# The output bias of an attention layer: from a product of ones to an add of a spread-out row

## Chip, cores and metric

The kernel runs on one core of one Trainium2 chip. The metric is the device time of one execution in microseconds (us); below, the time of a kernel is the median of several executions.

## What is computed

The reference is a small network on x of shape (8, 512, 512) with a context of shape (8, 512, 384), all in float32. It has four blocks, each added to its own input:

```
x = x + xattn0(layernorm(x), ctx)     # cosine similarities of two projections
x = x + ffn0(layernorm(x))            # quantised linear, depthwise conv, silu, linear
x = x + xattn1(layernorm(x), ctx)     # 16-head attention
x = x + ffn1(layernorm(x))            # gated feed-forward with squared relu
```

The change is in the third block, the 16-head attention (head size 32):

```
q = x @ w_q + b_q;  k = context @ w_k + b_k;  v = context @ w_v + b_v
weights = softmax(q k^T / sqrt(32))           # per head
out = weights @ v                              # 512 x 512 per batch
return out @ w_o + b_o
```

What is added to the residual stream is out @ w_o + b_o. The bias b_v passes through the softmax unchanged (the weights of a row add up to 1), so the kernel folds it in: it uses the row b_v @ w_o + b_o, 512 numbers, as the bias of the output projection, the same row for each of the 8 x 512 tokens.

## The kernel before

The program is one static instruction list for each engine. It is written out at build time by a planner, the class `Agenda`. Every piece of work is a Python generator, a task. A task yields what it wants next: an engine with a cost in us (`"P"` TensorE, `"V"` VectorE, `"W"` VectorE for operations that share a port with Pool, `"A"` ScalarE, `"G"` Pool, `"S"` SyncE, which issues all DMAs), a buffer of a `Kind`, an `Event`, or a plain waiting time. The planner keeps a clock of its own, hands each engine to the wanting task with the lowest rank (`ag.me.rank`, a due time in us), and so fixes the order of instructions on each engine. On the chip that order is never changed; an instruction whose data isn't there holds up all those behind it on its engine. If a cost changes or a step is added, the planner deals out the order of everything that follows anew.

Where a step could run on two engines, the task yields a list and the planner takes the one with the smaller burden: the work queued before it and its own cost, weighed by `LOAD`. For ranks over 600 the weights are 2.5 for VectorE and 0.7 for Pool. The helper `tensor` is the one that matters here; most of VectorE's and Pool's instructions carry line L363, that of the wrapper `Ported`:

```python
def tensor(out, a, b, op):
    n = a.free_size() / 512
    way = yield [("W", 0.07 + 0.53 * n), ("G", 0.16 + 1.07 * n)]
    (V, G)[way].tensor_tensor(out, a, b, op)
```

The planner treats `"W"` and `"G"` work as taking turns at one port (`Agenda.port`). `Ported` adds to a Pool operation a wait for VectorE's last `"W"` operation planned before it.

Buffers in the on-chip memory come from 25 pages of 8 KB per partition (`main`); in the traces they are all called "main". Product results lie in 8 banks of 128x512 floats ("bank").

The work runs in four phases, one for each block, which overlap by rank: the third is due from 620 us (`R3`), the fourth from 1260 us (`R4`). In the third phase:

- Queries, keys and values go through DRAM (qd, kd, vd) and come back as stacks per group of 4 heads. There are 32 such head groups (8 batches of 4), each due 19 us after the one before (`T3`).
- For each head group, `maxima` makes 16 products (L1424) whose row maxima VectorE takes (`maximum3`, a TENSOR_REDUCE from a bank); `attention` makes 16 products of scores (L1488); ScalarE takes their exponentials (L1496) into pairs of tiles of 128x1024.
- `summed` adds these pairs over the keys, with `tensor`: operations of 128x1024 on Pool or VectorE.
- `weigh` makes the products with the values (L1536) and `sums` those that add the sums over partitions (L1554). `finish3` divides (the sums pass through DRAM, sd) and splits the result into two parts for the projection, `split_sb`, again with `tensor` at 128x512.
- `projections3` makes the output projection: for each batch, and each of its 4 tiles of 128 tokens, it loads the residual tile x2 into `xt` (256 KB), takes a bank, and has `mac3` make 12 products of 128x512 into it (L456, L457, L458: each float32 factor is held as a high and a low part, and three of the four part products are made). A thirteenth product, L1611, adds the bias: a 128x128 matrix of ones times a tile whose row 0 is the bias's high part, row 1 its low part, and all other rows zero.
- `result3` then adds the bank to `xt` on VectorE and stores it to x3. `k3_xo` allows two tiles `xt` at a time, `b3_w` three banks.

The bias tile is made once, by `bias_row`: it waits for the weights w_o, loads b_o into one partition, makes b_v @ w_o with `mac3` into one row of a bank, adds the two, splits the row into its high and low part, and moves the low part from partition 0 to partition 1 by a DMA.

When the attention ends, the fourth phase loads x3 again (1 MB for a batch, `load_x`), normalises, and makes three 512x512 projections for each batch; its products are again L456 to L458.

Of the kernel before, what the change touches and what calls it, by code (L numbers as in the profile page):

```python
# [6 lines left out]
F32 = mybir.dt.float32  # L7
F32R = mybir.dt.float32r
# [4 lines left out]
ALU = mybir.AluOpType  # L13
# [3 lines left out]
P = 128  # L17
B, S, D = 8, 512, 512
NT = S // P
NC = D // P  # L20
# [354 lines left out]
def f32(ap):  # L375

    return ap.bitcast(F32)


def tile_kernel(tc, x, ctxT, vecs, bo, wvT, wtT, w1T, w2T, wqkvo, wrT, wkT, wv2T, out):  # L380
    nc = tc.nc
    A, T = nc.scalar, nc.tensor

    dram = tc.alloc_tile_pool(name="dram", bufs=1, space=bass.MemoryType.DRAM)
# [4 lines left out]
    vd = dram.tile([B, NG, P, NT, P], F32, name="vd")  # L389
    cd = dram.tile([B, 2, P, NCX, S], F32, name="cd")  # L390
    rd = dram.tile([B, 3, S], F32, name="rd")
    sd = dram.tile([NS, HG, S], F32, name="sd")
    qd = dram.tile([B, NG, 2 * HD, HG * S], F32, name="qd")

# [3 lines left out]
    def fixed(name, *shape, dtype=F32):  # L398
        return const.tile([P, *shape], dtype, tag=name, name=name, bufs=1)
# [7 lines left out]
    onesr = fixed("onesr", P, dtype=F32R)  # L407
# [11 lines left out]
    main = Memory(arena, "main", 25, 2048, 256, wide=0)  # L419
    psum = Memory(banks, "bank", 8, 512, 512)  # L420
    main.reserve = 2
    ag = Agenda()
    V, G = Ported(tc, ag, nc.vector), Ported(tc, ag, nc.gpsimd)
# [5 lines left out]
    def tok(t):  # L429
        return slice(t * P, (t + 1) * P)  # L430
# [19 lines left out]
    def mac3(ps, lhs, rhs, n, stop=True):  # L450

        for c in range(n):
            yield "P", 0.685
            lh, ll = lhs(c)
            rh, rl = rhs(c)
            T.matmul(ps, lh, rh, start=(c == 0), stop=False)  # L456
            T.matmul(ps, lh, rl, start=False, stop=False)  # L457
            T.matmul(ps, ll, rh, start=False, stop=(stop and c == n - 1))  # L458
# [14 lines left out]
# [5 lines that stand above are left out]
# [30 lines left out]
    def load(dst, src):  # L508
        yield "S", 0.5
        nc.sync.dma_start(dst, src)  # L510
        yield ag.transfer(src)

    store = load
# [124 lines left out]
    def parts(ww, c, cols):  # L638
        n = len(ww) // 2
        return ww[c][:, cols], ww[n + c][:, cols]  # L640
# [4 lines left out]
    ALL = slice(None)  # L645
# [665 lines left out]
    wq, wo, bo2 = [], [], []  # L1311
# [19 lines left out]
    def bias_row():  # L1331

        yield wo_done
        raw = small.kind(1, 2, NC, dtype=F32R)
        bvp = yield raw
        row = yield main.kind(1, D)
        both = yield main.kind(1, 2, D, dtype=F32R)
        yield from load(row[0:1], bo)
        bv3 = vec[:, COL["bv3"] : COL["bv3"] + NC]
        yield "V", 0.2  # L1340
        V.tensor_copy(bvp[:, 0], bv3)
        V.tensor_tensor(bvp[:, 1], bv3, f32(bvp[:, 0]), ALU.subtract)
        ps = yield b3_w
        yield from mac3(ps[0:1], lambda c: (bvp[:, 0, c : c + 1], bvp[:, 1, c : c + 1]), lambda c: parts(wo[0], c, ALL), NC)
        yield "V", 0.6
        V.tensor_tensor(row[0:1], ps[0:1], row[0:1], ALU.add)
        ag.give(ps, bvp)

        yield "G", 0.6
        G.memset(f32(both[:, 0]), 0.0)  # L1350
        yield "V", 0.9
        V.tensor_copy(both[0:1, 0], row[0:1])
        V.tensor_tensor(both[0:1, 1], row[0:1], f32(both[0:1, 0]), ALU.subtract)
        ag.give(row)

        yield from load(f32(both[1:2, 0]), f32(both[0:1, 1]))
        bo2.append(both)
        ag.set(bo_done)

# [238 lines left out]
    def projections3():  # L1598
        yield wo_done
        yield bo_done  # L1600
        for b in range(B):
            yield o_done[b]
            for t in range(NT):
                ag.me.rank = R3 + (b * NG + 4 + t) * T3
                xt = yield k3_xo
                yield from load(xt, x2[b, tok(t), :])
                ps = yield b3_w
                yield from mac3(ps, lambda c: (ohs[b, c][:, 0, tok(t)], ohs[b, c][:, 1, tok(t)]),
                                lambda c: parts(wo[0], c, ALL), NC, stop=False)
                yield "P", 0.23  # L1610
                T.matmul(ps, onesr, bo2[0][:, 0], start=False, stop=True)  # L1611
                ag.spawn(result3(b, t, ps, xt), ag.me.rank)
            ag.give(*(ohs[b, c] for c in range(NC)))
        ag.give(wo[0], bo2[0])

    def result3(b, t, ps, xt):
        yield "V", 0.60
        V.tensor_tensor(xt, ps, xt, ALU.add)
        ag.give(ps)
        yield from store(x3[b, tok(t), :], xt)  # L1620
        ag.give(xt)
        ag.set(x_done[3][b])

    def phase3():
        yield x_done[2][GQ]
        ag.spawn(norms3(), RQ)
        ag.spawn(split_weight(NC, D, wqkvo[:, 0:NC, :], k3_wrow, RQ, wq_done, wq, mixed=True), RQ)
        ag.spawn(queries(), RQ)
        yield x_done[2][G3]
        ag.spawn(stacks_made(), R3 - 5 * T3)  # L1630
        ag.spawn(stacks(), R3 - 3 * T3)
        ag.spawn(maxima(), R3 - 2 * T3)
        ag.spawn(values3(), R3 - T3)
        ag.spawn(attention(), R3)
        ag.spawn(projections3(), R3 + 4 * T3)
        ag.spawn(bias_row(), R3 + 3 * T3)
        yield q_done[0]
        ag.spawn(split_weight(NC, D, wqkvo[:, NC + 2 * NCX :, :], k3_wrow, R3 + 2 * T3, wo_done, wo), R3 + 2 * T3)
# [218 lines left out]
```

## Time and profile before

| what | value |
|---|---|
| median of 3 executions | 1591.54 us (1590.57 to 1591.71) |
| the profiled execution's own time | 1588.39 us |
| its span (first to last instruction) | 1586.6 us |
| granted TensorE clock, mean | 0.992 |
| busy over the span: PE / DVE / ACT / POOL | 97% / 78% / 70% / 40% |
| chain that ended last: PE / DVE / ACT / DMA / POOL | 66% / 16% / 6% / 3% / 1% |

PE is TensorE's products, PEld its weight loads, DVE VectorE, ACT ScalarE, POOL GpSimd. The chain is the sequence of work, followed back from the last instruction, each link released by the one before it. A row of a group of instructions reads: line, engine, operation, tiles written<-read, shape, count | busy us, mean ns of one | idle us of the engine just before them, and what ended it. The profiler's end of a product is modelled, so a product's duration is longer than the step to the next one. The profiled execution is one run and a little shorter than the median; durations are taken from it, times are compared as medians.

### The profile page before, as it was taken

Reading aid. Unit: us, or ns where it says so; the run is one execution under the profiler, and the core shown is the slowest. Engines: PE = TensorE matmul, PEld = TensorE weight load, DVE = VectorE, ACT = ScalarE, POOL = GpSimd, SP = SyncE. Lnnn points to the kernel's source line nnn. Section 1 sums busy time; section 2 is a strip of 40 time slices with the busy share of each in tenths; the row PEclk is TensorE's granted clock in tenths of the full one; section 3 lists DMA queues with packets and bytes.
Section 4 is the critical chain, followed back from the end, with each engine's and each line's share of the span. In section 5 each row is a group of like instructions: output and inputs, shape, how many; then the busy total and the mean of one; then the engine's idle time right before and its main releaser. Section 6 shows DMA issues by size and latency. Waiting matters only on the chain.

```text
span 1586.6 us, 22305 instructions
## 1 busy us (share of the span) xinstructions
PE 1531.6 (97%) x7552; PEld 984.5 (62%) x7552; DVE 1238.5 (78%) x2047; ACT 1105.5 (70%) x1809; POOL 638.4 (40%) x369
## 2 busy tenths in 40 slices
PE   7999999999999998999999999999999979999998
PEld 4565555665555565766765555555555557877886
DVE  6779989999989989878867887788987765554642
ACT  6788979888888877646756666667576674665661
POOL 1111100000000000326678879988888463543440
PEclk9999999999999999999999999999999989999999
DMA  9998424534453344786747565657665232121101
GB/s 327 327 370 279 154 80 145 171 124 153 138 186 105 129 156 144 252 261 211 208 152 197 156 178 151 181 143 211 166 162 134 62 120 80 53 71 63 60 27 54
DMA packets 133396, 251.49 MB, mean 159 GB/s; under 512 B 22689, under 2 KB 40481, under 8 KB 127138
## 3 DMA queue, kind: packets, MB, share of 16 engines
q1 hardware_dynamic: 133282, 250.06, 50.6%
q8 instruction: 60, 0.98, 0.3%
q14 instruction: 54, 0.44, 0.1%
HBM read 160.88 MB, written 88.34 MB: 157 GB/s over the span
## 4 chain that ended last, share of the span: by engine, by line
PE 66%; DVE 16%; ACT 6%; DMA 3%; issue 2%; POOL 1%; SPq 0%; ACTq 0%; DVEq 0%; POOLq 0%
DVE main L363 13%; PE bank L456 10%; PE bank L457 9%; PE bank L458 9%; PE bank L1488 7%; PE bank L1424 7%; PE bank L1536 6%; PE bank L1225 5%; DVE small L363 4%; PE bank L448 3%; PE bank L442 2%; PE bank L549 2%; PE bank L1554 2%; PE bank L1149 2%; DMA main<-x 1%
## 5 line engine op out<-in xcount | busy, mean ns | idle before, releaser
L363 POOL TENSOR_TENSOR main<-main,main 128x1024 f32<-128x1024 f32 (+2 forms) x290 | 535.6, 1870 | 387.6 <-DVE main L363 200.5
L363 DVE TENSOR_REDUCE small<-bank 128x1 f32<-128x512 f32 (+2 forms) x522 | 332.0, 677 | 97.5 <-PE bank L1424 95.2
L456 PE MATMUL bank<-main,main 128*128 128x512 f32 x846 | 376.0, 444 | 10.9 <-ACT main L1753 3.9
L1496 ACT ACTIVATE main<-bank 128x512 f32<-128x512 f32 x512 | 281.9, 601 | 105.8 <-PE bank L1488 103.3
L457 PE MATMUL bank<-main,main 128*128 128x512 f32 x880 | 347.6, 395 | 2.4 <-POOL main L363 1.6
L458 PE MATMUL bank<-main,main 128*128 128x512 f32 x842 | 332.0, 394 | 0.0
L363 DVE TENSOR_TENSOR main<-main,main 128x1024 f32<-128x1024 f32 (+5 forms) x226 | 273.1, 1222 | 26.1 <-ACT main L483 11.4
L363 POOL TENSOR_TENSOR small<-small,mhalf 128x4 f32<-128x4 f32 (+2 forms) x43 | 48.5, 1129 | 505.8 <-DVE small L363 364.1
L1488 PE MATMUL bank<-main,main 98*128 98x512 f32 x512 | 212.7, 418 | 2.5 <-DVE small L363 1.2
L1424 PE MATMUL bank<-main,main 96*128 96x512 f32 x512 | 210.7, 413 | 1.8 <-ACT main L1496 0.9
L456 PEld LDWEIGHTS bank<-main,main 128*128 128x128 f32 x846 | 160.7, 190 | 81.5 <-issue 19.6
L457 PEld LDWEIGHTS bank<-main,main 128*128 128x128 f32 x880 | 167.8, 191 | 36.1 <-issue 5.5
L363 DVE SCALAR_TENSOR_TENSOR main<-bank,vec,main 128x511 f32<-128x511 f32 x252 | 180.0, 743 | 8.6 <-ACT main L1155 7.7
L458 PEld LDWEIGHTS bank<-main,main 128*128 128x128 f32 x842 | 159.4, 189 | 35.6
L442 PE MATMUL bank<-main,main 128*128 128x512 fp8e4 x512 | 131.5, 380 | 6.7 <-ACT main L1131 5.5
L1488 PEld LDWEIGHTS bank<-main,main 98*128 98x128 f32 x512 | 96.3, 188 | 62.2 <-DVE small L363 15.0
L483 ACT CAST main<-main 128x512 fp32r<-128x512 f32 (+1 forms) x161 | 97.9, 626 | 39.7 <-POOL main L363 17.4
L1225 PE MATMUL bank<-main,main 128*128 128x512 fp8e4 x480 | 124.6, 384 | 0.3 <-DVE main L363 0.3
L1424 PEld LDWEIGHTS bank<-main,main 96*128 96x128 f32 x512 | 96.4, 189 | 42.2 <-ACT main L1496 10.6
L1536 PE MATMUL bank<-main,main 128*32 128x512 f32 x916 | 122.6, 596 | 0.0
L1155 ACT ACTIVATE main<-bank,vec 128x512 f32<-128x512 f32 x128 | 100.2, 787 | 10.2 <-PE bank L1149 10.1
L498 ACT ACTIVATE main<-main,small 128x512 f32<-128x512 f32 x98 | 78.2, 812 | 25.4 <-DVE small L363 14.5
(108 smaller groups left out, 2026.8 us busy)
## 6 DMA issues: line engine op xcount, KB each, us to landing
x<-main SPq DMA_DIRECT2D x96, 256.0 KB
main<-x SPq DMA_DIRECT2D x24, 1024.0 KB
kd<-main SPq DMA_DIRECT2D x32, 512.0 KB
main<-x SPq DMA_DIRECT2D x64, 256.0 KB
qd<-main SPq DMA_DIRECT2D x32, 512.0 KB
main<-kd SPq DMA_DIRECT2D x32, 512.0 KB
main<-qd SPq DMA_DIRECT2D x32, 512.0 KB
cd<-main SPq DMA_DIRECT2D x48, 256.0 KB
```

The lines of the kernel that those rows point to most:

```text
L363: ins = call(*args, **kwargs)
L442: T.matmul(ps, lhs(c), rhs(c), start=(c == 0), stop=(c == n - 1))
L456: T.matmul(ps, lh, rh, start=(c == 0), stop=False)
L457: T.matmul(ps, lh, rl, start=False, stop=False)
L458: T.matmul(ps, ll, rh, start=False, stop=(stop and c == n - 1))
L483: V.tensor_copy(out, src) if way == 0 else A.copy(out, src)
L1155: A.activation(g, ps, AF.Identity, bias=col("cb", f), scale=col("cw", 3 * f + 1))
L1225: T.matmul(po, qs[f // 2][:, f % 2, tok(t)], w2q[f // 8][:, f % 8, :], start=(f == 0), stop=(f == NF - 1))
L1424: T.matmul(ps, qs[0:96, j, tok(t)], ks[0:96, j, :], start=True, stop=True)
L1488: T.matmul(ps, ks[0:98, 2 * h + i, tok(k)], qs[0:98, 2 * h + i, :], start=True, stop=True)
L1496: A.activation(p, ps, AF.Exp, scale=qk_scale)
L1536: T.matmul(av[j * HD : (j + 1) * HD, :], vs[n][:, k, j * HD : (j + 1) * HD], ps[k, j // 2][0][:, j % 2, :], start=(k == 0), stop=(k == NT ...
```

## The change

The bias row is no longer multiplied in. `bias_row` stores the finished row (2 KB) to a DRAM tile `rb`, takes a buffer of 128x512, and loads the row from DRAM into all 128 partitions. In `projections3` the product L1611 is gone and the twelfth product closes the bank. A new task, `biased`, is spawned as soon as the tile of x2 is due to be loaded: it adds the spread-out row to `xt` with `tensor`, on VectorE or Pool, and sets an event. `result3` waits for that event before its own add.

```diff
+    rb = dram.tile([1, D], F32, name="rb")
...
         row = yield main.kind(1, D)
-        both = yield main.kind(1, 2, D, dtype=F32R)
         yield from load(row[0:1], bo)
...
         V.tensor_tensor(row[0:1], ps[0:1], row[0:1], ALU.add)
         ag.give(ps, bvp)

-        yield "G", 0.6
-        G.memset(f32(both[:, 0]), 0.0)
-        yield "V", 0.9
-        V.tensor_copy(both[0:1, 0], row[0:1])
-        V.tensor_tensor(both[0:1, 1], row[0:1], f32(both[0:1, 0]), ALU.subtract)
+        yield from store(rb, row[0:1])
         ag.give(row)
-
-        yield from load(f32(both[1:2, 0]), f32(both[0:1, 1]))
+        both = yield main.kind(1, D)
+        yield from load(both, rb.to_broadcast([P, D]))
         bo2.append(both)
         ag.set(bo_done)
...
                 xt = yield k3_xo
                 yield from load(xt, x2[b, tok(t), :])
+                ag.spawn(biased(xt, ready := Event()), ag.me.rank)
                 ps = yield b3_w
                 yield from mac3(ps, lambda c: (ohs[b, c][:, 0, tok(t)], ohs[b, c][:, 1, tok(t)]),
-                                lambda c: parts(wo[0], c, ALL), NC, stop=False)
-                yield "P", 0.23
-                T.matmul(ps, onesr, bo2[0][:, 0], start=False, stop=True)
-                ag.spawn(result3(b, t, ps, xt), ag.me.rank)
+                                lambda c: parts(wo[0], c, ALL), NC)
+                ag.spawn(result3(b, t, ps, xt, ready), ag.me.rank)
...
-    def result3(b, t, ps, xt):
+    def biased(xt, ready):
+        yield from tensor(xt, xt, bo2[0], ALU.add)
+        ag.set(ready)
+
+    def result3(b, t, ps, xt, ready):
+        yield ready
         yield "V", 0.60
         V.tensor_tensor(xt, ps, xt, ALU.add)
```

## The prediction, made before the changed kernel was run

> **What bounds the kernel now.** I read the page's first part, then where the removed products lie, then the stage around them in four views: busy time by stage, the chain that ended last, groups by shape, and TensorE's timeline.
>
> ```profile
> PE 1531.6 (97%) x7552; PEld 984.5 (62%) x7552; DVE 1238.5 (78%) x2047; ACT 1105.5 (70%) x1809; POOL 638.4 (40%) x369
> ```
>
> Next the answer for the source line of the product of ones (durations in ns, first and last start in us):
>
> ```profile
> L1611 PE MATMUL bank<-main,onesr x32: 394/399/498, 849.9 to 1327.1; 128*128 128x512 f32 x32
> ```
>
> There are 32 of them, from 850 to 1327 us. So the change acts in the last 740 us, and the stages there are unlike each other (columns: length, then busy time and count for PE, PEld, DVE, ACT, POOL):
>
> ```profile
> 850.00:1260.00 410.00, 406.49 (x2163) 230.31 (x2162) 334.18 (x501) 268.59 (x516) 344.08 (x170) 1.00 0.60 160
> 1260.00:1300.00 40.00, 31.65 (x137) 19.10 (x136) 29.21 (x35) 28.66 (x51) 24.41 (x17) 0.87 0.35 107
> 1300.00:1330.00 30.00, 28.78 (x129) 22.82 (x128) 15.34 (x22) 15.52 (x27) 12.88 (x10) 1.00 0.30 97
> 1330.00:1587.00 257.00, 248.42 (x1126) 201.68 (x1125) 126.91 (x202) 137.98 (x234) 99.81 (x71) 1.00 0.16 55
> ```
>
> Pool is at 40% over the span, but at 84% (344 of 410) in the attention stage, where 27 of the 32 products lie. The average hides that. The chain in that stage:
>
> ```profile
> by line: PE bank L1488 20.3%; PE bank L1424 18.4%; PE bank L1536 17.4%; PE bank L456 6.6%; DVE small L363 6.4%; PE bank L457 5.5%; PE bank L458 5.5%; PE bank L1554 5.2%; DVE main L363 3.3%; POOL main L363 3.0%; DMA main<-kd 3.0%; issue 2.2%
> ```
>
> The PE lines make 79%, VectorE 9.7%, Pool 3.0%. What VectorE and Pool do there, by shape:
>
> ```profile
> L363 POOL TENSOR_TENSOR main<-main,main 128x1024 f32<-128x1024 f32 x106 | 253.4, 2407 | 33.8 <-ACT main L1496 21.3 <-DVE main L363 10.1 <-PE bank L1536 1.3
> L363 DVE TENSOR_REDUCE small<-bank 128x1 f32<-128x512 f32 x379 | 238.0, 678 | 66.5 <-PE bank L1424 66.1
> L363 DVE TENSOR_TENSOR main<-main,main 128x1024 f32<-128x1024 f32 x33 | 68.2, 2072 | 4.6 <-POOL main L363 3.1 <-ACT main L1496 1.5
> L363 POOL TENSOR_TENSOR main<-main,main 128x512 fp32r<-128x512 f32 x27 | 35.0, 1297 | 10.5 <-DVE main L363 6.1 <-PE bank L1536 1.3 <-DVE small L363 1.3
> L363 POOL TENSOR_TENSOR main<-main,main 128x512 f32<-128x512 f32 x22 | 28.3, 1285 | 18.0 <-DMA main<-sd 11.4 <-DVE main L363 3.5 <-DVE small L363 3.0
> L363 DVE TENSOR_TENSOR main<-bank,main 128x512 f32<-128x512 f32 x26 | 17.7, 679 | 2.6 <-PE bank L1611 2.6
> L363 POOL TENSOR_TENSOR main<-main 128x512 f32<-128x512 f32 x3 | 3.9, 1301 | 0.0
> L363 DVE TENSOR_TENSOR main<-main,main 128x512 fp32r<-128x512 f32 x2 | 3.5, 1752 | 0.0
> L363 DVE TENSOR_TENSOR main<-main 128x1024 f32<-128x1024 f32 x1 | 1.2, 1220 | 0.0
> L363 DVE TENSOR_TENSOR main<-main,main 128x512 f32<-128x512 f32 x1 | 0.7, 680 | 0.0
> ```
>
> Two things matter. First, VectorE's maxima (the TENSOR_REDUCE row) wait 66 us for products: they are ready before the products are, so TensorE is the bound there. Second, a sum of two SBUF tiles of 128x1024 takes 1.22 us on VectorE undisturbed, but 2.07 us on average here: beside a busy Pool it waits. The program treats the two as sharing one port (`Agenda.port`; `Ported` makes a Pool operation wait for VectorE's last turn). By that reckoning the port's turns in this stage are Pool's 344.1 plus 33 x 1.22 = 40.3 us: **384 of 410 us, 94%**. So there is a second, nearly full resource beside TensorE.
>
> **The change, part by part.**
>
> *The products.* A matmul is listed with 0.40 us, but the next one starts sooner:
>
> ```profile
> 928.04 0.39 PE L1424 MATMUL bank<-main,main 96*128 96x512 f32 x1
> 928.27 0.39 PE L1611 MATMUL bank<-main,onesr 128*128 128x512 f32 x1
> 928.50 0.27 PE L1439 MATMUL bank<-ident,small 128*16 128x128 f32 x1
> ```
>
> The step is 0.23 to 0.24 us; I take 0.235. All 32 are worth 7.5 us, not the 13 us that 32 x 0.40 would make. In the attention stage 27 x 0.235 = 6.3 us, times the 79% of the chain that is PE: 5.0 us. The one in 1260 to 1300, where PE's busy time falls to 79% and the next phase waits for its first loads, is worth nothing. The four after 1300 stand in a stage bound by products: 0.9 us, less the tenth of it that is not PE, 0.8. Gain: 5.8 us, between 0 (if the gaps swallow it) and 7.5.
>
> *The adds.* 32 adds of two 128x512 tiles come instead, through `tensor`, which lets the planner choose the engine. Operations of this size through the same helper stand in the rows above 27 + 22 + 3 times on Pool (1.29 us) and 2 + 1 times on VectorE (0.68 alone). By that split 26 of the stage's 27 go to Pool: 26 x 1.29 + 0.7 = 34 us of port turns. The result's own add (679 ns) reads a bank and one tile and is there before and after. So 384 + 34 = 418 us of turns are wanted in a stage of 410 that should shrink to 405. They don't fit. The planner will answer by putting more of the 128x1024 sums on VectorE: each one moved saves 2.40 - 1.22 = 1.18 us of port and costs VectorE 2.07 us. Port and VectorE are equally full when 418.6 - 1.18k = 334.9 + 2.07k: k = 26, both at 388 us. At today's fill (384 of 410) a stage that needs 388 lasts 414 us. So the stage gets **3.9 us longer** rather than 5.0 shorter. Ends: 5.0 shorter less 1.0 (26 x 1.29 us at Pool's 3% of the chain) where all of it is hidden; with nothing moved and the port without a gap, 418.6, which is 8.6 longer; with half as many moved (403 us) at today's fill, 20 longer. I take the balanced value, since the planner counts both queues and the port.
>
> [...]
>
> [...] All 27 adds on VectorE would make 18 us of turns instead of 34.
>
> *The wait for the load.* `biased` starts when the tile of x2 is due, earlier than the result's add did, so Pool or VectorE may now stand waiting for a DMA, with Pool's sums or VectorE's maxima queued behind. Nearest row, an operation that waits for its own 256 KB load:
>
> ```profile
> L363 DVE SCALAR_TENSOR_TENSOR main<-bank,small,main 128x512 f32<-128x512 f32 x28 | 20.8, 744 | 3.2 <-DMA main<-x 3.0
> ```
>
> That is 0.11 us each, 3 us for 27, of which the 12.7% of the chain that VectorE and Pool hold is 0.4 us. If each waited for 2 us it would be 7. The `ready` event costs nothing while the add ends within a tile's twelve products (12 x 0.235 = 2.8 us at least); behind one 2.4 us sum it is 0.9 us late, and then holds one of three banks of `b3_w`.
>
> *The bias row.* One memset, two copies on one partition and the small DMA go; a 2 KB store and a 256 KB load come, so SP issues three DMAs instead of two (0.3 to 0.4 us more, with loads of kd and qd behind it). The row is made by 707 us and first used at 850 us: 143 us of cover, cost nothing. Without cover it would be two landings. The buffer shrinks from 4 KB to 2 KB per partition; I put that at nothing.
>
> *The tail.* The last five adds fall after 1260, where Pool is at 61% and then 43%; one or two may lie on the path from the last head group to the next phase: 0.5 us.
>
> Sum: +3.9 - 0.8 + 0.4 + 0.5 = +4.0 us. The profiled execution took 1588.39 us (span 1586.6), 3.2 below the median of 1591.54; the difference is carried to the median: **1595.5 us**. About 0.2%, 3.2 us, is what a measurement can tell from no change.
>
> **Rivals.**
> *Faster: the products were the bound and the adds hide.* -5.0 + 1.0 - 0.8 + 0.4 + 0.5 = -3.9: 1587.6. For it: 79% of the chain is PE, Pool 3%. Against it: the port's 94%. It decides if fewer than 4 of the 26 adds on Pool come onto the path (5.0 / 1.29).
> *No change: PE's gaps swallow the step.* TensorE then waits for the same exponentials and maxima: 1591 to 1592. Against it: maxima wait for PE, not the other way.
> *The next phase starts at another moment.* Its first load (8.66 us on the chain at 1269) may move, since the order of all engines is planned anew: 1586 or 1598.
>
> **How the numbers follow.** Port too full 0.50 (own range 1592.5 to 1604: same 0.10, slower 0.40); hidden adds 0.30 (1584 to 1590: faster 0.24, same 0.06); swallowed step 0.10 (faster 0.02, same 0.08); moved start 0.10 (half and half). Together faster 0.31, same 0.24, slower 0.45. The range is 1584 to 1604: from the whole PE gain to two thirds of the way to the 20 us case.
>
> **What would show it.** No L1611 row, 32 more adds of 128x512, most on Pool; in the attention stage more than 33 sums of 128x1024 on VectorE, their mean at or above 2.07 us, Pool and VectorE with a larger share of the chain, and the last product of attention later than 1260. I am wrong if that stage shortens by about 5 us with Pool above 90% busy, or if the stage stays and the time moves elsewhere.

## The result, and the profile after

The changed kernel takes 1600.91 us (median of 8 runs) where the kernel before takes 1591.62 us in the runs beside it (also 8). The ratio over these runs is **1.0047, 95% interval 1.0034 to 1.0060**: on 1591.5 us that is 7.5 us slower (5.4 to 9.6). (The two medians alone give 1.0058, inside the interval.) The forecast was 4.0 us slower.

The profiled execution took 1602.58 us, its span is 1600.6 us. This is 14.0 us more than the span before, which is twice what the ratio says. The two must not be subtracted as they stand. The instruction streams of both kernels are the same up to about 704 us, yet at the first product of the maxima (690 us) this execution is already 6.9 us later: a difference of two executions, not of two programs. From here on, shifts are given after taking out the offset at that product; 14.0 - 6.9 = 7.1 us is then left, and agrees with the ratio.

From the page of the changed kernel, busy time and instructions:

```profile
PE 1539.6 (96%) x7520; PEld 983.8 (61%) x7520; DVE 1267.8 (79%) x2066; ACT 1101.7 (69%) x1809; POOL 647.8 (40%) x379
```

TensorE has 32 products fewer (7552 to 7520) and is still busy 8 us longer. By stage (length, then busy time and count of PE, PEld, DVE, ACT, POOL, then granted clock, DMA share, GB/s):

```profile
720.00:850.00 130.00, 128.94 (x645) 85.68 (x643) 100.61 (x178) 84.71 (x152) 84.30 (x42) 0.96 0.63 190
850.00:1260.00 410.00, 404.77 (x2128) 223.85 (x2128) 352.88 (x523) 263.47 (x508) 352.65 (x180) 1.00 0.61 161
1260.00:1300.00 40.00, 34.70 (x170) 17.94 (x168) 30.38 (x37) 28.67 (x54) 20.12 (x12) 0.91 0.40 120
```

In the attention stage VectorE works 19 us more (334 to 353), Pool 9 us more (344 to 353), and TensorE makes 35 products fewer in the same 410 us, where 27 were taken out. (The windows are those of before; by the offset of 6.9 us they hold work that lies a little earlier.) The start of the attention (720 to 850) runs at a granted clock of 0.96. The chain of waits in the attention stage:

```profile
by line: PE bank L1484 17.2%; PE bank L1420 16.2%; PE bank L1532 15.2%; DVE small L363 11.4%; DVE main L363 7.9%; PE bank L457 5.3%; PE bank L1550 5.1%; POOL main L363 4.8%; PE bank L458 4.5%; PE bank L459 4.4%; issue 3.1%; ACT main L1492 2
```

The PE lines now hold 68% instead of 79%, VectorE 19% instead of 10%, Pool 4.8% instead of 3.0%. The groups behind it, from the groups by shape in that stage:

```profile
L363 POOL TENSOR_TENSOR main<-main,main 128x1024 f32<-128x1024 f32 x105 | 250.2, 2398 | 30.6 <-DVE main L363 15.6 <-ACT main L1492 13.4 <-DVE small L363 1.4
L363 DVE TENSOR_REDUCE small<-bank 128x1 f32<-128x512 f32 x387 | 240.9, 675 | 50.0 <-PE bank L1420 49.8
L363 DVE TENSOR_TENSOR main<-main,main 128x1024 f32<-128x1024 f32 x39 | 75.4, 1935 | 0.5 <-ACT main L1492 0.2
L363 POOL TENSOR_TENSOR main<-main,main 128x512 f32<-128x512 f32 x37 | 47.3, 1285 | 8.7 <-DVE main L363 8.6
L363 DVE TENSOR_TENSOR main<-main,main 128x512 f32<-128x512 f32 x7 | 9.3, 1322 | 0.2 <-DMA main<-sd 0.2
L363 DVE TENSOR_TENSOR main<-bank,main 128x512 f32<-128x512 f32 x25 | 17.2, 687 | 6.1 <-PE bank L459 4.6 <-POOL main L363 0.8 <-PE bank L1484 0.3
```

Over the whole attention, adds and sums of 128x512 in float32 went from 35 on Pool and 1 on VectorE to 59 and 9. The adds themselves are 27 on Pool and 5 on VectorE: f2 below, which has the order of the changed kernel without the adds, shows 32 and 4. An operation of this shape on VectorE takes 1.32 us here (the row of 7, all beside operations of Pool); in the same trace 12 of them with no operation of Pool under way take 0.68 to 0.69. VectorE's maxima wait 50 us for products instead of 66: VectorE has less slack.

### The profile page after: what moved, and what is told of

Same layout as the page of the kernel before. It is cut to its first block, busy times and chain, and to the rows that moved or that the text cites. A ratio compares the mean times of both kernels' runs of the same rounds, so it can differ in the third digit from the quotient of the medians.

```text
span 1600.6 us, 22295 instructions
## 1 busy us (share of the span) xinstructions
PE 1539.6 (96%) x7520; PEld 983.8 (61%) x7520; DVE 1267.8 (79%) x2066; ACT 1101.7 (69%) x1809; POOL 647.8 (40%) x379
## 4 chain that ended last, share of the span: by engine, by line
PE 62%; DVE 19%; ACT 6%; DMA 3%; issue 2%; POOL 2%; SPq 0%; DVEq 0%; ACTq 0%; POOLq 0%
DVE main L363 14%; PE bank L457 10%; PE bank L458 9%; PE bank L459 9%; PE bank L1484 6%; PE bank L1420 6%; PE bank L1532 5%; PE bank L1226 5%; DVE small L363 5%; PE bank L449 3%; PE bank L443 2%; PE bank L550 2%; PE bank L1550 2%; POOL main L363 2%; PE bank L1150 2%
## 5 line engine op out<-in xcount | busy, mean ns | idle before, releaser
L363 POOL TENSOR_TENSOR main<-main,main 128x512 fp32r<-128x512 f32 (+2 forms) x309 | 563.6, 1846 | 394.0 <-DVE main L363 111.8
L363 DVE TENSOR_TENSOR main<-main,main 128x1024 f32<-128x1024 f32 (+4 forms) x244 | 300.7, 1245 | 27.3 <-ACT main L484 11.4
L1420 PE MATMUL bank<-main,main 96*128 96x512 f32 x512 | 214.9, 422 | 3.3 <-DVE small L363 1.9
```

What stands on the lines that cost most here:

```text
L363: ins = call(*args, **kwargs)
L1420: T.matmul(ps, qs[0:96, j, tok(t)], ks[0:96, j, :], start=True, stop=True)
```

## The experiments

All times are ratios to the kernel before in runs on the same chip (the kernels e, f and g ran in three batches, each on its own chip). Because single executions differ as shown above, each experiment's trace was also laid against the one of before, with the offset at the first maxima taken out. The shifts in us (one execution each) at five marks: the first product of the scores, the first product that adds the sums over partitions in the first and in the last head group, and the first and the last output store of the fourth phase:

| kernel | first scores | first sums | last sums | first output | last output |
|---|---|---|---|---|---|
| after | +2.4 | +5.4 | +7.1 | +7.3 | +6.9 |
| after, adds not issued, same order (f2) | +2.4 | +4.7 | +0.2 | +1.9 | +1.5 |
| before, products not issued, same order (f1) | 0.0 | 0.0 | -1.2 | -1.6 | -1.7 |
| whole change, old order at the start (g3) | 0.0 | +2.0 | +7.3 | -1.7 | +2.3 |
| before, only the order new (e4) | 0.0 | +1.9 | +7.6 | +6.5 | +10.0 |

The order of e4 is that of before up to about 948 us; its +1.9 at the first sums is thus no effect of a program (at 720.5 us its clock is half for 6.8 us, in the profile before it is full there). Some 2 to 3 us at that mark are the doubt of one execution. The +2.4 at the first scores is no such doubt: the five profiles whose `bias_row` has the change's steps alone show 2.38 to 2.41, all others 0.0.

### One part at a time, order dealt anew

Three kernels, each with one part of the change, and one that changes nothing but a number the planner is told.

The changed kernel without its adds:

```diff
-                ag.spawn(biased(xt, ready := Event()), ag.me.rank)
...
-                ag.spawn(result3(b, t, ps, xt, ready), ag.me.rank)
+                ag.spawn(result3(b, t, ps, xt), ag.me.rank)
```

> The changed kernel without its 32 adds of the bias (the output bias is left out); the row is still spread through DRAM, the products of ones are gone. Theory A (the adds on VectorE and Pool cost what the products saved and more): without them the saving of the products is left, ratio to before about 0.9965 (-5.8 us), and the start of the attention (717 to 745 us) is no slower than in before. Theory B (the loss is made at the start of the attention, by the new order around the bias row, and by the halved TensorE clock that follows): the granted clock near 0.5 at about 727 us is there again, first sums of the attention some 5 us late, ratio between 0.999 and 1.001.

Measured: 0.9999 (0.9987 to 1.0012). Without the adds the loss is gone. But the removed products bring no gain either.

The kernel before without its products:

```diff
-                                lambda c: parts(wo[0], c, ALL), NC, stop=False)
-                yield "P", 0.23
-                T.matmul(ps, onesr, bo2[0][:, 0], start=False, stop=True)
+                                lambda c: parts(wo[0], c, ALL), NC)
```

> The kernel before without its 32 products of ones and nothing in their place (the output bias is left out); the bias row is made as before. This prices the products alone. Theory A: -5.8 us, ratio 0.9963. Theory C (any edit deals out the order of the whole attention anew, and that alone moves the time by several us either way): anything between -12 and +6 us, with no relation to the 7.5 us of products that are gone.

Measured: 1.0014 (1.0001 to 1.0026). Less work on TensorE, and if anything slower: something else than the work counts here.

The changed kernel with the product kept as well:

```diff
+        two = yield main.kind(1, 2, D, dtype=F32R)
...
+                yield "P", 0.23
+                T.matmul(ps, onesr, bo2[0][:, 0], start=False, stop=True)
```

> The changed kernel with the products of ones kept as well, so the bias is added twice (once by a product, once by the add). This prices the adds and the spread row alone. Theory A: the port has 384 us of turns in 410 already, so the adds cost 8 to 14 us, ratio 1.005 to 1.009. Theory B: the loss stands at the start of the attention, about 5 us, and the adds themselves under 3 us: ratio about 1.005 with the delay already there at 760 us. Theory C: no relation, ratio 0.998 to 1.012.

Measured: 1.0063 (1.0049 to 1.0077). With the product kept it is 0.16% slower than the change, 2.5 us, with intervals that overlap.

The kernel before, with the same instructions, the planner told 0.25 us for the product instead of 0.23:

```diff
-                yield "P", 0.23
+                yield "P", 0.25
```

> The kernel before with the same instructions, but the product of ones is entered in the planner with 0.25 us instead of 0.23, so that the order from the first projection (850 us) on is dealt out anew. Theories A and B: the same time as before within 0.2%, since no work is added or taken. Theory C: it moves by 0.2% or more in either direction, and the difference arises after 850 us.

Measured: **1.0056 (1.0041 to 1.0072)**. Not one instruction is added or removed; the order differs from about 948 us on. So a new order alone is worth as much as the whole effect to be explained, and the three runs before it can't price an edit to less than some 9 us. The parts had to be tried again with the order held.

### One part at a time, order held

The kernel before; the planner still sees the product, but it is not issued:

```diff
-                                lambda c: parts(wo[0], c, ALL), NC, stop=False)
+                                lambda c: parts(wo[0], c, ALL), NC)
                 yield "P", 0.23
-                T.matmul(ps, onesr, bo2[0][:, 0], start=False, stop=True)
```

> The kernel before, the order of all engines held: the planner still counts 0.23 us for each product of ones, but the product isn't issued (the output bias is left out). This is the price of the products without a new order. If products bound the attention: -5.8 us, ratio 0.9963. If TensorE's gaps swallow the step: under 1.5 us, ratio 0.999 or above. Theory C (the new order made the difference in the run without products) expects the first.

Measured: 0.9990 (0.9974 to 1.0006), so the 32 products are worth 1.6 us (from 4.1 saved to 1.0 lost), not their step of 7.5. In the trace 1.2 us of them lie in the attention, 0.6 us after it.

The changed kernel; the planner still sees the adds, but they are not issued:

```diff
     def biased(xt, ready):
-        yield from tensor(xt, xt, bo2[0], ALU.add)
+        yield [("W", 0.60), ("G", 1.23)]
         ag.set(ready)
```

> The changed kernel with its order held: the planner still gives each add its place on VectorE or Pool, but the add isn't issued (the output bias is left out). This is the price of the adds without a new order. Theory A (the port is too full): 6 to 10 us below the changed kernel, ratio to before 0.998 to 1.001. Theory C (the new order is what costs): less than 3 us below the changed kernel, ratio 1.003 or above.

Measured: 1.0002 (0.9988 to 1.0016). Against the changed kernel at 1.0047 this is the price of the 32 adds in their own order: 0.45%, **7.2 us**, about 3 us either way by the two intervals. In the traces it is 7.0 us at the last sums, 5.4 at the end. The 128x1024 sums in its attention stage:

```profile
L363 POOL TENSOR_TENSOR main<-main,main 128x1024 f32<-128x1024 f32 x103 | 244.9, 2393 | 48.5 <-DVE main L363 22.5 <-ACT main L1492 20.2 <-DVE small L363 3.0
L363 DVE TENSOR_TENSOR main<-main,main 128x1024 f32<-128x1024 f32 x44 | 73.8, 1680 | 2.8 <-ACT main L1492 2.7
```

With the same order, Pool idles 18 us more before these sums than in the changed kernel (48.5 against 30.6), and VectorE does one in 1.68 us instead of 1.94. What the adds take is Pool's slack, and 0.26 us more for each of VectorE's sums of 128x1024. In the chain of this stage TensorE holds 84% without the adds and 68% with them.

### Is it the port?

Three kernels make the whole change in the order of the kernel before, with the add put in where the planner doesn't know of it. The first and the third differ in the operands of the add alone; the second also issues it earlier, ahead of the products. In all three `bias_row` issues the store and the spreading load within the steps that the planner knew, into the old buffer `both`. First the add on VectorE, two operands in the on-chip memory:

```diff
+        V.tensor_tensor(xt, xt, f32(bo2[0][:, 0]), ALU.add)
         V.tensor_tensor(xt, ps, xt, ALU.add)
```

> The whole change in the order of before: row spread through DRAM, products not issued, and each add issued on VectorE just ahead of the result's own add, without the planner counting it. Theory A: 32 adds of 0.7 to 2 us on VectorE, which wait for Pool's turns: 3 to 8 us dearer than the run without products in the same order, ratio 0.998 to 1.002. Theory C: they cost at most 3 us, ratio 0.996 to 0.9985, faster than before.

Measured: 1.0377 (1.0353 to 1.0401), 60 us. The adds' group in the attention stage, then the stage itself:

```profile
L363 DVE TENSOR_TENSOR main<-main,main 128x512 f32<-128x512 f32 x23 | 37.6, 1636 | 0.0
```

```profile
850.00:1260.00 410.00, 379.54 (x1896) 204.23 (x1896) 326.94 (x473) 241.17 (x457) 323.64 (x156) 0.95 0.57 150
```

An add of this form, which takes 0.68 to 0.69 us in the profile before where no operation of Pool is under way (12 of them), takes 1.64, with no idle time before it: the delay is inside the instruction. VectorE's total is even lower than before (327 of 410 us, since fewer head groups pass in this time), so VectorE isn't full. TensorE makes 1896 products in the stage, and its clock falls to 0.95; the kernel before without the product of ones (f1) makes 2148:

```profile
850.00:1260.00 410.00, 405.31 (x2148) 225.39 (x2148) 334.53 (x502) 268.07 (x515) 346.08 (x171) 1.00 0.60 161
```

The same on Pool, ahead of the products:

```diff
                 yield from load(xt, x2[b, tok(t), :])
+                G.tensor_tensor(xt, xt, f32(bo2[0][:, 0]), ALU.add)
                 ps = yield b3_w
```

> As the one before, but each add is issued on Pool when its tile of x2 is due, without the planner counting it. Theory A: 32 times 1.29 us on a Pool that is busy for 84% of the attention, sums and parts behind it late: ratio 1.002 to 1.008. Theory C: Pool's adds fall into its waits, ratio 0.996 to 0.999.

Measured: 1.0140 (1.0119 to 1.0160), 22 us. Pool's operations of this shape hardly get longer (1337 ns on average, x44; 1285 before), but Pool goes to 370 of 410 us, 90%, and from 3.0% of the chain in this stage to 17.0%:

```profile
850.00:1260.00 410.00, 391.47 (x2032) 214.64 (x2024) 333.00 (x483) 255.08 (x491) 370.02 (x190) 1.00 0.59 157
```

On VectorE again, but the bias is added to the bank in place, so that one operand is the bank:

```diff
+        V.tensor_tensor(ps, ps, f32(bo2[0][:, 0]), ALU.add)
         V.tensor_tensor(xt, ps, xt, ALU.add)
```

> As the run with the adds on VectorE in the order of before (ratio 1.038), but the bias is added to the product's bank in place (one tile and one bank read, the bank written), then the bank to the residual as ever. VectorE does the same number of operations; none of them reads two SBUF tiles. Theory A (the port): the added operation takes 0.7 us instead of 1.6, and most of the 60 us go: ratio 1.000 to 1.010. If it is VectorE's load and not the port: 0.7 to 1.6 us each is still on the path, ratio above 1.015.

Measured: 1.0073 (1.0055 to 1.0091), 12 us.

```profile
L363 DVE TENSOR_TENSOR bank<-bank,main 128x512 f32<-128x512 f32 x25 | 17.2, 689 | 0.0
```

Same engine, same place, same shape, same order as the first of the three: 689 ns instead of 1636, and 48 of the 60 us are gone. Only the place of one operand, and with it of the result, differs. The traces say the same operation by operation. In the first of the three, VectorE's 33 operations of this form take 0.63 to 0.69 us where no operation of Pool runs meanwhile (5 of them), and 1.65 us on average, up to 4.41, where one does (28). The adds to the bank take 0.67 to 0.70 us with Pool (28) and without (4). Nor is it a wait that the program makes: `Ported` makes Pool wait only for `"W"` steps, and both adds are issued in a `"V"` step. **For an add on VectorE it is shown**: beside Pool it is dear, 1.65 us instead of 0.63 to 0.69, where both of its operands lie in the on-chip memory, and costs no more than alone (0.67 to 0.70 us) where one lies in a bank. That much the planner's port stands for; what in the chip makes VectorE's operation longer there, no run shows.

For an add on Pool it is not shown. The second kernel's 22 us can come from Pool's own time, 32 operations more on an engine that was busy for 84% of the stage; no run here tells that from turns with VectorE.

The same in-place add, known to the planner:

```diff
-        yield "V", 0.60
+        yield "V", 1.25
+        V.tensor_tensor(ps, ps, bo2[0], ALU.add)
         V.tensor_tensor(xt, ps, xt, ALU.add)
```

> The changed kernel with the bias added to the bank in place on VectorE, counted by the planner in one step with the result's add (1.25 us), and no add on VectorE or Pool before it. Theory A: about as the changed kernel without its adds (0.9999) plus 32 x 0.7 us x VectorE's 10 to 20% of the chain, ratio 1.001 to 1.004, below the changed kernel's 1.0047. Theory C (luck of the order): 0.996 to 1.008.

Measured: 1.0027 (1.0014 to 1.0041). It has no event, no second task and no port turn, and is 0.20% below the changed kernel; the intervals just overlap (1.0034 to 1.0041). In a newly dealt order, after what 0.25 for 0.23 us did, that difference is not settled.

### The order of the start

Two kernels of the whole change, with other orders. First, the planner is given the steps and the buffer of the old `bias_row`, so that the attention starts as before; the adds stay as in the change:

```diff
-        yield from store(rb, row[0:1])
+        yield "G", 0.6
+        yield "V", 0.9
         ag.give(row)
-        both = yield main.kind(1, D)
-        yield from load(both, rb.to_broadcast([P, D]))
+        yield "S", 0.5
+        nc.sync.dma_start(rb, row[0:1])
+        nc.sync.dma_start(f32(both[:, 0]), rb.to_broadcast([P, D]))
+        yield ag.transfer(f32(both[0:1, 1]))
```

> The whole change, adds placed by the planner, but the bias row's steps are kept in the planner's books as in before, so that the order up to the first projection (850 us) is that of before. If the start of the attention carries 2 to 4 us of the loss: its first scores and sums are as in before, and the ratio falls to 1.002 to 1.0035. If the start is only the gated clock of single runs: ratio 1.0045 as the change.

Measured: **0.9992 (0.9977 to 1.0008)**. The whole change, 32 adds included, costs nothing that can be measured in this order. But the reason is not only the start. By the table it saves 2.4 us at the first scores and 3.4 at the first sums, yet at the last sums it is as late as the changed kernel: +7.3. It gets 9 us back between there and the first output, and loses 4 of them again by the last. Its loads of in_wrT, a weight of the fourth phase, are issued from 1255 us on (offset taken out), in the changed kernel from 1272 us, before from 1269 us. That this earlier place is the reason isn't shown: e4 issues the first of them at 1235 us, and its first output is 6.5 us late. The same 20 us of the handover (about 1290 to 1310 of before), in the changed kernel and then in this one:

```profile
1297.00:1317.00 20.00, 15.15 (x64) 11.51 (x64) 13.15 (x14) 12.87 (x23) 18.77 (x13) 0.91 0.24 71
```

```profile
1294.50:1314.50 20.00, 19.63 (x91) 15.36 (x90) 13.08 (x14) 15.42 (x28) 15.73 (x12) 1.00 0.21 68
```

TensorE makes 91 products there instead of 64 (before, from 1290 to 1310 us: 84). In the changed kernel's chain a piece stands at this place that waits for a weight of the next phase:

```profile
1308.28 2.91 DMA main<-in_wv2T
```

Second, the changed kernel with the adds' measured times told to the planner (0.68 and 1.29 us instead of 0.60 and 1.23):

```diff
-        yield from tensor(xt, xt, bo2[0], ALU.add)
+        way = yield [("W", 0.68), ("G", 1.29)]
+        (V, G)[way].tensor_tensor(xt, xt, bo2[0], ALU.add)
```

> The changed kernel with the same instructions, but the planner is told 0.68 and 1.29 us for the adds (as the trace has them) instead of 0.60 and 1.23, so that the order is dealt out anew from about 850 us on. Theory A: within 0.3% of the changed kernel, still slower than before, ratio 1.002 to 1.008. Theory C with the luck as large as in the replanned kernel of before (1.0056): anywhere from 0.999 to 1.012.

Measured: 1.0045 (1.0029 to 1.0061), as the change itself. Its last sums come at +7.7, its first output at +11.7. So better costs for the adds don't mend it.

No kernel tried is reliably faster than the one before. The whole change in the order above (0.9992) can't be told from it.

## Why the prediction was right, and where not

The sign and the likeliest case came true: the adds cost more than the products bring, and 1591.5 + 7.5 = 1599.0 us lies in that case's own range. Of its cause, a port too full, the runs show that an add on VectorE with two operands in the on-chip memory takes 1636 ns beside a busy Pool, and with one in a bank 689; for the 27 adds on Pool it stays joined with Pool's own load. That the sign came true has luck in it: the same change in another order measured 0.9992, and the kernel before, with nothing but its order dealt anew, 1.0056. Step by step:

- **The products: mis-sized.** Forecast -5.8 us, measured -1.6, and the interval (4.1 saved to 1.0 lost) leaves the forecast out. The step of 0.235 us is right, and the 0.8 after 1300 was about right (0.6). The failing factor is the 79%: the chain's PE share was taken as the part of a removed product that the end would feel. In the traces it is 1.2 of 6.3 us in the attention, 19%. A chain says which work ended last as things stood; it doesn't say that the next one behind it is far. The rival "PE's gaps swallow the step" was right about this term, though not about the whole.
- **The adds: right order of size.** 8.9 us (from -5.0 to +3.9) against 7.2, about 3 either way, by the pair with the order held, so the size is not refuted. The way it came about was wrong in part: the split was nearly right (27 of 32 on Pool; forecast 26 of the stage's 27), but only 13 more of the 128x1024 sums on VectorE over the attention (38 to 51), 6 of them in the stage (33 to 39), where the balance wanted 26. The turns at the planner's port grew instead: the time in which Pool or an operation of VectorE on two such operands is under way went from 381 of 410 us to 394 (93% to 96%), not to 388; in the order of the changed kernel without the adds (f2) it is 370. The planner evens out by its own weights, not by times on the chip.
- **The bias row: wrong in its reason.** "Cost nothing" rested on 143 us of cover for the data. The data was in time; but changing the steps and the buffer had the planner deal out the start of the attention anew. The first scores come 2.4 us later with it, and 0.0 with the old steps. Whether this reaches the end isn't shown. The two kernels with the order held differ in the whole order, not only in the start: 1.0002 less 0.9990, 1.9 us (by the traces 3.2), and the ratios' own intervals are wider than that. At the last sums the one with the new start (f2) is only 0.2 us later than before.
- **The wait for the load and the tail:** 0.4 and 0.5 us, too small to be seen. From the last sums to the end nothing is added (+7.1 to +6.9).
- **The sum:** -1.6 + 1.9 + 7.2 = +7.5, by differences that add up by construction; forecast -5.8 + 8.9 + 0 + 0.9 = +4.0. The gain of the products was put too high by 4.2 us and the new order, which the sum put at nothing, too low by 1.9; the adds were put too high by 1.7 and the small terms by 0.9: in all 3.5 too low.
- **The rival of the moved start** was given 0.10 and deserved more: two orders of the same change differ by 8.8 us (1.0047 and 0.9992), and in the traces by 9 us at the first output of the fourth phase, though both come to the last sums equally late. In the change as it was made the handover added nothing.
- **The marks:** no product of ones, the adds mostly on Pool, more 128x1024 sums on VectorE, a larger share of VectorE and Pool in the chain: all as forecast. The mean of those sums should have been 2.07 us or more and fell to 1.94; the mark was badly chosen, because the mean changes with the order alone: 2.07 us before and 1.68 in f2, neither with the 32 adds. With the order held it rose as it should, 1.68 to 1.94. "Later than 1260" was a poor mark too: the last product of the attention lies at 1272.6 us before already; 1286.8 after is 7.3 later, offset out.

Open: why one order gives the fourth phase's weights an earlier place than another, and so how much of the 7.5 us belongs to the change and how much to the order it happened to get. The order of e4, with no change in the work, is also 7.6 us late at the last sums. What is shown is the price of the adds in the one order they came with, and that an add on VectorE with both operands in the on-chip memory is dear beside Pool (1.65 us, against 0.63 to 0.69 without an operation of Pool).

## What to carry to other kernels

One engine can be slowed by another while neither is full: with VectorE busy for 327 of 410 us and Pool for 324, an add on VectorE of two tiles in the on-chip memory took 1.65 us here beside an operation of Pool and 0.63 to 0.69 otherwise. Where a trace shows this, add up the time of both engines' operations of that kind before moving work there, and look for another form of the operation, as the add to the bank in place (0.67 to 0.70 us with Pool and without). A product removed from a TensorE that waits on others in between can be worth far less than its step, even where TensorE holds 79% of the chain: here 32 were worth 1.6 us, not 7.5. Where a planner deals out the order, price an edit with the order held, by not issuing what was planned; a newly dealt order alone moved this kernel by 0.56%.

## What was not expected of the hardware

**The granted clock halved where TensorE had not been idle for more than 0.46 us at a time in the 40 us before.** At the start of the attention the changed kernel's windows of 10 us read:

```profile
717.00:727.00 10.00, 9.33 (x42) 6.12 (x41) 9.76 (x17) 4.86 (x9) 1.27 (x1) 1.00 1.02 315
727.00:737.00 10.00, 9.60 (x25) 5.55 (x27) 8.62 (x15) 6.82 (x12) 2.71 (x2) 0.51 0.59 137
737.00:747.00 10.00, 10.00 (x58) 6.09 (x61) 8.86 (x19) 4.88 (x9) 9.29 (x5) 0.98 0.21 67
```

For 10.2 us from 727.1 on the granted clock is half; a product's step is then 0.43 us instead of 0.23. The profile before has no such stretch there. TensorE's timeline just before:

```profile
722.22 1.03 PE L1420 MATMUL bank<-main,main 96*128 96x512 f32 x3
723.21 0.63 PE L550 MATMUL bank<-ident,main 128*128 128x128 f32 x4
723.59 2.65 PE L1420 MATMUL bank<-main,main 96*128 96x512 f32 x6
726.70 0.50 PE L1420 MATMUL bank<-main,main 96*128 96x512 f32 x1 [0.46 <-DVE small L363]
```

Six products of the maxima take 2.65 us from 723.59 on; at the full step they would take 1.6 (5 x 0.235 and the 0.40 of the last). The next one waits 0.46 us for VectorE. TensorE is fed thinly here; what halves the clock isn't shown. Twelve of the fourteen profiles have a stretch of 3.4 to 10.2 us at this place, and it isn't the change's doing: e4, which has the order of before up to 948 us, has one, while before and f1 have none. The add on VectorE in the old order has eleven such stretches between 850 and 1260 us, 44 us in all; before has none there. Leaving out the ends of the runs, a stretch lasts 3.4, 6.8 or 10.2 us in all these profiles.

**Two executions of the same instructions can be 7 us apart before any of them differs.** The profile after is 5.8 us behind the profile before by 115 us, among the first loads, and 6.9 us at 690 us. Anyone who subtracts two spans here reads 14 us instead of 7.
